# Gated cross-attention with RMSNorm: the next quad's scores behind the attention products, transposed blocks of 32 columns, two weight queues

## The chip, the cores and the metric

The kernel runs on one core of a Trainium2 chip. The core has five engines that run side by side: TensorE (matrix products), VectorE, ScalarE, GpSimd, and SyncE, which only issues transfers. They share one on-chip memory (SBUF); TensorE writes its products to a small second memory (PSUM), from which VectorE and ScalarE read them. The profile calls the engines PE (with PEld for the loading of weights), DVE, ACT, POOL and SP. The metric is the device time of one execution in microseconds.

## The reference, cut to what matters

```python
# x: (8, 1024, 1024)   ctx_1024: (8, 64, 512)
# W_mem: (1024, 512)   W_gate: (1024, 2048)   b_gate, norm_w: (1024,)
memory_proj = jnp.einsum('bme,de->bmd', memory, W_mem)
scores = jnp.einsum('bnd,bmd->bnm', hidden_states, memory_proj) / jnp.sqrt(jnp.float32(D))
attn = jax.nn.softmax(scores, axis=-1)
memory_context = jnp.einsum('bnm,bmd->bnd', attn, memory_proj)
gate_input = jnp.concatenate([hidden_states, memory_context], axis=-1)
gate = jax.nn.sigmoid(jnp.einsum('bnf,df->bnd', gate_input, W_gate) + b_gate)
fused = hidden_states + gate * memory_context
return fused * jax.lax.rsqrt(jnp.mean(jnp.square(fused), -1, keepdims=True) + EPS) * norm_w
```

All is float32. The large work is the gate's product with the part of `W_gate` that meets x, called W1 (1024 x 1024): 8192 rows of x go through it. The other half, W2, meets the memory context. Since the context is attn times the projected memory, W2 is applied once to the projected memory (512 rows in all), and attention is then taken over that product.

## The kernel before, in words

The 8192 rows of x are worked in 16 quads of 512 rows (four tiles of 128); two quads make a batch (`QPB`). The kernel has a start and a main loop.

**The start.** W_mem (`wm`), the memory (`memq`), W2 (eight tiles `w2_0` to `w2_7`, the profile's `w`) and W1 (two tiles `w1_0`, `w1_1`, also `w`) are loaded. TensorE transposes the memory (`pt`, copied to `memT` by VectorE and ScalarE), then forms the projected memory transposed, `pm`, in 32 products over four steps k of W_mem's rows; `mpT` are its copies in SBUF. `mg_product` then multiplies it with W2, `pg`, in seven products of half-size blocks (a Strassen scheme of one level, the sums of blocks `w2_sum`, `mp_step`, `mg_sum` on VectorE and GpSimd). The projected memory is stored as `mpd` and `mgd[0]`, the product with W2 as `mgd[1]`; `load_mp` and `load_mg` bring each batch's part back as `mpb` and `mg`, and `add_bias` adds the gate's bias to `mg` by an accumulating transfer that GpSimd issues.

**The main loop.** A quad of x is loaded as `xq` (`load_xq`, SyncE's queue) in an order in which VectorE's transpose of 32x32 blocks gives x transposed; `transpose_x` makes the tiles `a11`, `a12`, `a21`, `a22` (row half, column half), eight instructions a quad. The product of the quad with W1 is a Strassen scheme of two levels: seven outer products in the order 1, 6, 7, 5, 4, 2, 3 (`ORDER`), each of seven inner products A, B, C, D, A (second part), E, F. One inner product takes a *slot*; a quad has 49. `outer_s` (VectorE) makes the left operands S1 to S4 of the outer level, `inner_s` (GpSimd) those of the inner level, tile `l2`, the profile's `l`, in two buffers and two parts for each outer product. The right operands, sums of blocks of W1, are made once (`outer_sum`, `inner_sum`: tiles `t`, `it`). Inner products are evacuated to `u` and `gate` by VectorE (`fin`), ScalarE (copies) and GpSimd (`pre`).

The scores of a quad (`scores`) are 16 pairs of products in 64-column tiles, `psT` in PSUM bank `sc`; ScalarE copies them to `sT`, TensorE transposes them (`transpose_scores`), `softmax_a` and `softmax_b` make the softmax, and `transpose_attn` turns it to `attnT`. The last four outer products (5, 4, 2, 3) have an attention block between their second A and E: eight pairs of products in 64-row tiles, whose one half gives the context (`pc`), and whose other half adds the gate's part from the context to the inner products A, F, E and D. Then follow sigmoid (ScalarE), `gated` (VectorE), `residual` (an accumulating transfer issued by GpSimd), `square` (ScalarE), `norm` (VectorE) and the store.

**What sets the order.** Each engine works its instructions in the order in which they were written (`pin` keeps it). The order is written out by hand: `at(slot, ...)` puts a call ahead of the inner product of that slot, `mid((q, o), ...)` puts it behind the attention block of outer product o of quad q, ahead of E. `plan(q)` does this for a quad:

```python
at(t0 + 7, scores, q)
at(t0 + 7, outer_s, q, 3)
at(t0 + 7, outer_s, q, 4)
at(t0 + 9, transpose_scores, q)
```

So the scores of quad q stood between the outer products 1 and 6 of the quad itself. S3 overwrites `a21`, which the scores read. SyncE's and GpSimd's queues are in order too: an instruction that waits holds up what is written behind it.

Of the kernel before, what the change touches and what calls it, by code (L numbers as in the profile page):

```python
# [15 lines left out]
P = 128  # L16
# [4 lines left out]
def tile_gated_cross_attention_rmsnorm(  # L21
# [7 lines left out]
    norm_w: bass.AP,  # L29
    out: bass.AP,  # L30
):

# [28 lines left out]
    nc = tc.nc  # L64
    B, N, D = x.shape
    M, E = mem.shape[1:]
    QT = 4 * P
    QPB = N // QT
    NQ = B * QPB
    BM = B * M  # L70
    KD = D // P
    KE = E // P
# [9 lines left out]
    apool = ctx.enter_context(tc.tile_pool(name="apool", bufs=1))  # L82
    rot = ctx.enter_context(tc.tile_pool(name="rot", bufs=2))
    small = ctx.enter_context(tc.tile_pool(name="small", bufs=1))
# [4 lines left out]
    pin = tc.keep_in_program_order  # L89

    def mm(o, lhsT, rhs, start, stop):
        pin(nc.tensor.matmul(o, lhsT, rhs, start=start, stop=stop, skip_group_check=True))  # L92

    def tt(eng, o, a, b, op):
        pin(eng.tensor_tensor(o, a, b, op))  # L95

    def load(o, i):
        pin(nc.sync.dma_start(o, i))

    def t4k(pool, shape, tag, name):  # L100
        return pool.tile(shape, F32, tag=tag, name=name)

    def rows_by_chunk(w, n):

        return w.rearrange("(p j) f -> p j f", j=n)

    def chunks(t, n):

        return t.rearrange("p s e -> p (s e)").rearrange("p (m j) -> p j m", j=n)

    banks = [f"b{i}" for i in range(5)]

    def bank(n, shape, name):
        return ps.tile(shape, F32, tag=banks[n % 5], name=name)
# [11 lines left out]
    wm = t4k(xqpool, [P, KE, D], "xq", "wm")  # L126
# [3 lines left out]
        load(memq[g], memr[g])  # L130
    load(wm[:, 1, :], wmr[:, 1, :])
    load(wm[:, 2:, :], wmr[:, 2:, :])
    w2r = rows_by_chunk(w_gate_t[D:, :], KD)
    w2 = []
    for k in range(KD):
        t = t4k(*((gpool, [P, D], "gate") if k < 7 else (apool, [P, D], "s4")), f"w2_{k}")
        load(t, w2r[:, k, :])
        w2.append(t)

    w1 = [const.tile([P, 4, D], F32, name=f"w1_{h}") for h in range(2)]
    for h in range(2):
        load(w1[h], rows_by_chunk(w_gate_t[:D, :], KD)[:, 4 * h : 4 * h + 4, :])
    nw_sb = const.tile([P, D], F32, name="nw_sb")
    load(nw_sb, norm_w.partition_broadcast(P))
    xq = {}
# [17 lines left out]
    def w1_place(o):  # L165

        if o in (5, 6, 4):
            outer_b[o] = const.tile([P, 4, H], F32, tag=f"t{o}", name=f"t{o}")
        inner_t[o] = const.tile([P, 3, 2, C], F32, tag=f"it{o}", name=f"it{o}")
# [17 lines left out]
    def transpose_mem(g):  # L187

        cols = slice(g * (BM // 2), (g + 1) * (BM // 2))
        for k in range(KE):  # L190
            for r in range(2):
                n = 2 * g + r
                pin(
                    nc.tensor.transpose(
                        pt[k][:, n * P : (n + 1) * P], memq[g][:, r, k * P : (k + 1) * P], ident
                    )
                )
            o = memT[k // 2][:, k % 2, cols]
            pin((nc.scalar.copy if k % 2 else nc.vector.tensor_copy)(o, pt[k][:, cols]))

    pt = [bank(4, [P, BM], "pt0")]
    pt += [ps_ctx.tile([P, BM], F32, tag="ctx", name=f"pt{k}") for k in (1, 2)]
    pt += [ps.tile([P, BM], F32, tag="sc", name="pt3")]
    for g in range(2):
        transpose_mem(g)
    pm = [bank(j, [P, BM], f"pm{j}") for j in range(5)]
    pm += [ps_ctx.tile([P, BM], F32, tag="ctx", name=f"pm{j}") for j in (5, 6)]
    pm += [ps.tile([P, BM], F32, tag="sc", name="pm7")]
    for k in range(KE):
        for j in range(KD):  # L210
            mm(
                pm[j],
                chunks(wm[:, k : k + 1, :], KD)[:, j],
                memT[k // 2][:, k % 2, :],
                k == 0,
                k == KE - 1,
            )


    def outer_sum(o, a, b, k=slice(0, 4)):  # L220
        tt(nc.vector, outer_b[o][:, k], outer_b[a][:, k], outer_b[b][:, k], ALU.subtract)

    def inner_sum(eng, o, n):
        s, a, b = ((T1, R12, R11), (T2, R22, T1), (R12, R22, R12), (T4, R21, T2))[n]
        tt(eng, w_op(o, s), w_op(o, a), w_op(o, b), ALU.subtract)

    def inner_sums(eng, o):
        w1_place(o)
        for n in range(4):
            inner_sum(eng, o, n)  # L230
# [3 lines left out]
    A, S, L2, O = {}, {}, {}, {}  # L234
# [4 lines left out]
    def transpose_x(q, t, half):  # L239

        key = q, t // 2, half
        if key not in A:
            A[key] = t4k(
                apool, [P, KH, 2 * P], f"a{t // 2 + 1}{half + 1}", f"a{t // 2 + 1}{half + 1}_{q}"
            )
        r = t % 2
        pin(
            nc.vector.transpose(  # L248
                A[key][:, :, r * P : (r + 1) * P],
                chunks(xq[q][:, 4 * t : 4 * t + 4, :], KD)[:, half * KH : (half + 1) * KH],  # L250
            )
        )

# [122 lines left out]
    KH = KD // 2  # L376
# [8 lines left out]
    def w2_sum(eng, o, a, b):  # L385
        for k in range(KH):
            tt(eng, o[k], a[k], b[k], ALU.subtract)
# [1 line left out]
    w2_sum(nc.vector, t1, b12, b11)  # L389
    w2_sum(nc.vector, t2, b22, t1)  # L390
    w2_sum(nc.gpsimd, b12, b22, b12)
    w1_place(5)
    outer_sum(5, 7, 1)
    inner_sums(nc.vector, 1)


    mpT = [[t4k(apool, [P, KH, HM], f"a{r + 1}{h + 1}", f"mpT{r}{h}") for h in range(2)] for r in range(2)]
    for j in range(KD):
# [8 lines left out]
    def mp_step(eng, tag, pool, a, b, op):  # L407
        t = t4k(pool, [P, KH, HM], tag, f"mp_{tag}")
        tt(eng, t, a, b, op)
        return t  # L410

    def store_mp(g):

        r, n = g // 2, g % 2
        mpq = const.tile([P, 4, Q4], F32, tag=f"it{(4, 6, 2, 3)[g]}", name=f"mpq{g}")
        for h in range(2):
            pin(
                nc.vector.transpose(
                    chunks(mpq, KD)[:, h * KH : (h + 1) * KH],
                    mpT[r][h][:, :, n * P : (n + 1) * P],  # L420
                )
            )
        for i in range(4):
            load(
                mgd[0, g * P : (g + 1) * P, i * Q4 : (i + 1) * Q4].rearrange(
                    "(s c) e -> c s e", c=32
                ),
                mpq[32 * i : 32 * (i + 1), :, :],
            )
# [28 lines left out]

    s1 = mp_step(nc.vector, "s1", apool, m21, m22, ALU.add)
    s2 = mp_step(nc.vector, "s2", apool, s1, m11, ALU.subtract)  # L460
    outer_sum(7, 3, 7)
    w1_place(7)
    s3 = mp_step(nc.gpsimd, "junk", small, m11, m21, ALU.subtract)
# [9 lines left out]
    for g in (2, 3, 0, 1):  # L473
        store_mp(g)
# [4 lines left out]
    for t in range(4):  # L479
        transpose_x(0, t, 0)  # L480
# [17 lines left out]
    for t in range(2):  # L498
        transpose_x(0, t, 1)
# [7 lines left out]
    for t in (2, 3):  # L507
        transpose_x(0, t, 1)
# [11 lines left out]
    def at(slot, fn, *args):  # L520
        due.setdefault(slot, []).append(lambda: fn(*args))

    def mid(key, fn, *args):
        beside.setdefault(key, []).append(lambda: fn(*args))
# [5 lines left out]
    def plan(q):  # L530
        t0 = SLOTS * q
        nxt = q + 1 < NQ
        order = [o for o, _ in ORDER]
        for i, o in enumerate(order):
            for part, t in ((0, 1), (1, 5)):
                if i + 1 < len(order):
                    at(t0 + 7 * i + t, inner_s, q, order[i + 1], part)
                elif nxt:
                    at(t0 + 7 * i + t, inner_s, q + 1, order[0], part)
        at(t0 + 7, scores, q)  # L540
        at(t0 + 7, outer_s, q, 3)
        at(t0 + 7, outer_s, q, 4)
        at(t0 + 9, transpose_scores, q)
        at(t0 + 10, softmax_a, q)
        at(t0 + 13, softmax_b, q)
        at(t0 + 18, transpose_attn, q)
        at(t0 + 21, attn_difference, q)
        if not nxt:
            at(t0 + 5, load_last)
            return  # L550
        at(t0 + 2, load_xq, q + 1)
        for t in (2, 3):
            mid((q, 5), transpose_x, q + 1, t, 0)
            mid((q, 2), transpose_x, q + 1, t, 1)
        for i, t, half in ((36, 0, 0), (38, 1, 0), (43, 0, 1), (45, 1, 1)):
            at(t0 + i, transpose_x, q + 1, t, half)
        mid((q, 3), outer_s, q + 1, 1)
        mid((q, 3), outer_s, q + 1, 2)
        if (q + 1) % QPB == 0:
            at(t0 + 10, load_mp, (q + 1) // QPB)  # L560
            at(t0 + 49, load_mg, (q + 1) // QPB)
        if q % QPB == 0:
            at(t0 + 8, add_bias, q // QPB)

    for o in (2, 3):
        w1_place(o)
# [246 lines left out]
    for q in range(NQ):  # L813
        plan(q)
        for o, ext in ORDER:
            outer_product(q, o, ext)
# [29 lines left out]
```

## Time and profile before

| what | value |
| --- | --- |
| time, median of 3 runs | 981.03 us (980.83 to 981.19) |
| span of the profiled run | 979.4 us |
| busy: PE, DVE, POOL, ACT | 99%, 84%, 75%, 33% |
| transposes of x on DVE (L248) | 128, 1098 ns each |
| transposes mpq on DVE (L418) | 8, 1101 ns each |
| score products psT | 512 records, 58.8 us |
| attention products pc | 512 records, 127.4 us |
| weight loads: of wm for pm, of most other products | 314 ns, 190 ns |
| transfers w from in_w_gate_t, SyncE's queue | 8 of 512 KB, 2 of 2048 KB; median 11.0 and 15.6 us from issue to landing |

How to read it: each product of the program leaves two records on PE, and a product's record lasts longer than its distance to the next, since products are pipelined. So the busy share of PE says that it always had work, not how well it was used; distances between starts of records say what a product costs. The busy shares are means over the whole span. A row of a group gives busy time in all and the mean of one. Idle time of an engine that isn't on the chain that ended last costs nothing.

### The profile page before, as it was taken

What the parts mean: (1) busy time and instruction counts of PE and PEld (TensorE: products, weight loads), DVE (VectorE), ACT (ScalarE), POOL (GpSimd) and SP (SyncE); (2) the same over time, 40 slices, a digit from 0 to 9 for tenths busy, and PEclk for the clock granted to TensorE, in tenths of its full rate; (3) what the DMA queues carried; (4) which work ended last, traced back from release to release, by engine and by line L of the source; (5) the groups of instructions that cost most, each with busy time, mean ns of one, the idle gap of its engine ahead of it and who ended that gap; (6) DMA issues with size and microseconds to landing.
All of it is one profiled execution on the core that took longest, in us unless ns stands there. A gap on an engine that the chain in (4) does not pass through costs nothing.

```text
span 979.4 us, 14277 instructions
## 1 busy us (share of the span) xinstructions
PE 964.8 (99%) x4938; PEld 769.8 (79%) x4938; DVE 820.4 (84%) x1487; ACT 324.9 (33%) x602; POOL 730.5 (75%) x881
## 2 busy tenths in 40 slices
PE   9999999999999999999999999999999999999995
PEld 6546888888887888888887888888887888888873
DVE  3888788979797988979797988979797988979787
ACT  1100234151433334151433334151433334151434
POOL 3366877878787877878787877878787877878772
PEclk9999999999999999999999999999999999999998
DMA  9865264482918374482918374482818364482612
GB/s 372 258 153 145 39 120 107 103 188 62 186 65 165 108 141 106 102 190 65 183 65 164 111 138 105 107 184 66 182 65 168 110 136 104 108 184 68 169 65 86
DMA packets 71255, 128.32 MB, mean 131 GB/s; under 512 B 12432, under 2 KB 49296, under 8 KB 70928
## 3 DMA queue, kind: packets, MB, share of 16 engines
q1 hardware_dynamic: 61760, 93.34, 35.3%
q0 software_dynamic: 9280, 33.56, 18.5%
q8 instruction: 39, 0.64, 0.3%
q10 hardware_dynamic: 144, 0.52, 0.2%
q14 instruction: 32, 0.26, 0.1%
HBM read 87.56 MB, written 39.85 MB: 130 GB/s over the span
## 4 chain that ended last, share of the span: by engine, by line
PE 96%; DVE 2%; DMA 1%; issue 0%; ACT 0%; POOL 0%; DVEq 0%; ACTq 0%
PE kA L92 20%; PE pc L92 12%; PE kE L92 11%; PE kF L92 10%; PE kD L92 10%; PE kC L92 10%; PE kB L92 10%; PE psT L92 6%; PE pg L92 5%; PE pm L92 3%; DVE gate L95 1%; DMA memq<-in_mem 1%; DVE gate L660 0%; PE pa L342 0%; PE sc L316 0%
## 5 line engine op out<-in xcount | busy, mean ns | idle before, releaser
L95 POOL TENSOR_TENSOR gate<-gate,u 128x256 f32<-128x256 f32 x336 | 270.4, 835 | 115.7 <-DVE u L95 110.1
L582 ACT ACTIVATE gate<-gate 128x512 f32<-128x512 f32 x128 | 79.0, 629 | 400.1 <-DVE gate L95 400.1
L95 POOL TENSOR_TENSOR l<-a 128x256 f32<-128x256 f32 x128 | 128.9, 1007 | 60.4 <-DVE a L95 55.8
L248 DVE STREAM_TRANSPOSE a<-xq 128x512 f32<-128x512 f32 x128 | 137.9, 1098 | 4.0 <-DMA xq<-in_x 4.0
L92 PE MATMUL pc<-mg,attnT 64*128 64x256 f32 x512 | 127.4, 389 | 0.0
L611 DVE SCALAR_TENSOR_TENSOR gate<-gate,ss,nw_sb 128x512 f32<-128x512 f32 x120 | 126.0, 1060 | 1.1
L92 PE MATMUL kD<-it,l 128*128 128x256 f32 x448 | 115.0, 379 | 0.0
L92 PE MATMUL kB<-it,l 128*128 128x256 f32 x448 | 115.0, 379 | 0.0
L92 PEld LDWEIGHTS pc<-mg,attnT 64*128 64x128 f32 x512 | 90.6, 186 | 29.7 <-issue 21.2
L92 PE MATMUL kA<-w,a 128*128 128x256 f32 x384 | 98.7, 379 | 0.4 <-ACT u L726 0.4
L92 PEld LDWEIGHTS kD<-it,l 128*128 128x128 f32 x448 | 85.1, 190 | 11.6
L92 PEld LDWEIGHTS kB<-it,l 128*128 128x128 f32 x448 | 85.1, 190 | 11.6
L95 DVE TENSOR_TENSOR gate<-gate,pc 128x512 f32<-128x512 f32 x128 | 87.0, 680 | 5.8 <-ACT gate L582 5.8
L95 POOL TENSOR_TENSOR l<-s 128x256 f32<-128x256 f32 x96 | 75.7, 789 | 10.8 <-PE kF L92 10.7
L92 PEld LDWEIGHTS kA<-w,a 128*128 128x128 f32 x384 | 71.6, 190 | 10.2 <-ACT u L726 0.8
L726 ACT COPY u<-kA 128x256 f32<-128x256 f32 x112 | 40.5, 362 | 102.1 <-PE kA L92 99.9
L92 PE MATMUL kE<-it,a 128*128 128x256 f32 x256 | 69.0, 392 | 0.0
L95 DVE TENSOR_TENSOR u<-u,kB 128x256 f32<-128x256 f32 x112 | 45.5, 406 | 28.1 <-PE kB L92 24.9
L92 PE MATMUL kA<-t,s 128*128 128x256 f32 x256 | 67.4, 386 | 0.0
L92 PE MATMUL kC<-w,l 128*128 128x256 f32 x256 | 65.7, 379 | 0.0
L92 PE MATMUL kF<-w,l 128*128 128x256 f32 x256 | 65.7, 379 | 0.0
L596 ACT ACTIVATE junk<-gate 128x1024 f32<-128x1024 f32 x60 | 63.5, 1059 | 2.1 <-DMA gate<-in_x 1.2
(123 smaller groups left out, 1996.6 us busy)
## 6 DMA issues: line engine op xcount, KB each, us to landing
xq<-in_x SPq DMA_DIRECT2D x64, 512.0 KB, 9.6
gate<-in_x POOLq DMA_DIRECT2D x60, 512.0 KB, 7.8
out<-gate SPq DMA_DIRECT2D x60, 512.0 KB, 2.6
w<-in_w_gate_t SPq DMA_DIRECT2D x8, 512.0 KB, 11.0
w<-in_w_gate_t SPq DMA_DIRECT2D x2, 2048.0 KB, 15.6
mg<-mgd SPq DMA_DIRECT2D x16, 256.0 KB, 4.0
mpd<-mpT SPq DMA_DIRECT2D x4, 512.0 KB, 3.8
mgd<-mpq SPq DMA_DIRECT2D x16, 128.0 KB, 2.6
```

Of the source, the lines that this page charges most:

```text
L92: pin(nc.tensor.matmul(o, lhsT, rhs, start=start, stop=stop, skip_group_check=True))
L95: pin(eng.tensor_tensor(o, a, b, op))
L248: nc.vector.transpose(A[key][:, :, r * P : (r + 1) * P], chunks(xq[q][:, 4 * t : 4 * t + 4, :], KD)[:, half * KH : (half + 1) * KH],)
L582: pin(nc.scalar.activation(g, g, AF.Sigmoid))
L596: nc.scalar.activation(junk, O[q, t], AF.Square, accum_out=ss[:, t % 2 : t % 2 + 1])
L611: nc.vector.scalar_tensor_tensor(g[:, cols], g[:, cols], rstd[:, t % 2 : t % 2 + 1], nw_sb[:, cols], ALU.mult, ALU.mult,)
L726: pin(nc.scalar.copy(p1, kb["A"]))
```

## The change

It has three parts, and some moves of the sums around them.

1. *Scores.* The scores of quad q + 1 are computed behind the attention block of outer product 3 of quad q, so that the products in 64-column tiles follow those in 64-row tiles without full-size products between. Quad 0 keeps the old place. S3 and S4 move to slots 4 and 16 (they no longer need to follow the scores at slot 7), `add_bias` to slot 4, and the last two transposes of x from slots 43, 45 to 42, 43.
2. *Blocks of 32 columns.* The block transposes took every eighth column; now they take 32 columns in a row, and the rows of W1 and W2 are loaded in the order that fits. The projection needs W_mem's columns in that order too, so VectorE copies W_mem to four tiles `wmp` in the new order, from which TensorE reads packed weights.
3. *Two queues.* Each tile of W1 and W2 is loaded in four transfers of 32 partitions, two by SyncE's and two by GpSimd's queue. A one-column copy on GpSimd (`warm`) makes its transfers wait until W_mem's second part has landed. The sums for the right operands of the outer products 5 and 1 move behind the first sums of the projected memory.

```diff
-    def rows_by_chunk(w, n):
-        return w.rearrange("(p j) f -> p j f", j=n)
-    def chunks(t, n):
-        return t.rearrange("p s e -> p (s e)").rearrange("p (m j) -> p j m", j=n)
+    def rows_by_chunk(w):
+        return w.rearrange("(i j r) f -> i r j f", i=4, r=32)
+    def by_queue(o, w, j):
+        for i in range(4):
+            eng = nc.sync if i < 2 else nc.gpsimd
+            pin(eng.dma_start(o[32 * i : 32 * (i + 1)], w[i][:, j, :]))
...
+    warm = t4k(small, [P, 1], "warm", "warm0")
+    pin(nc.gpsimd.tensor_copy(warm, wm[:, 1, 0:1]))
...
-        load(t, w2r[:, k, :])
+        by_queue(t, rows_by_chunk(w_gate_t[D:, :]), k)
...
-        load(w1[h], rows_by_chunk(w_gate_t[:D, :], KD)[:, 4 * h : 4 * h + 4, :])
+        by_queue(w1[h], rows_by_chunk(w_gate_t[:D, :]), slice(4 * h, 4 * h + 4))
...
+    def order_wm(k):
+        t = t4k(apool, [P, KD, P], ("a11", "a12", "a21", "a22")[k], f"wmp{k}")
+        pin(
+            nc.vector.tensor_copy(
+                t.rearrange("p j (i r) -> p j i r", r=32),
+                wm[:, k, :].rearrange("p (i j r) -> p j i r", i=4, r=32),
+            )
+        )
+        wmp.append(t)
+    order_wm(0)
...
     for g in range(2):
         transpose_mem(g)
+    for k in range(1, KE):
+        order_wm(k)
...
-                chunks(wm[:, k : k + 1, :], KD)[:, j],
+                wmp[k][:, j, :],
...
-                A[key][:, :, r * P : (r + 1) * P],
-                chunks(xq[q][:, 4 * t : 4 * t + 4, :], KD)[:, half * KH : (half + 1) * KH],
+                A[key][:, :, r * P : (r + 1) * P].rearrange("p j (s c) -> p s j c", c=32),
+                xq[q].rearrange("p s (j r) -> p s j r", r=32)[
+                    :, 4 * t : 4 * t + 4, half * KH : (half + 1) * KH, :
+                ],
...
     w2_sum(nc.gpsimd, b12, b22, b12)
-    w1_place(5)
-    outer_sum(5, 7, 1)
-    inner_sums(nc.vector, 1)
...
     s2 = mp_step(nc.vector, "s2", apool, s1, m11, ALU.subtract)
+    w1_place(5)
+    outer_sum(5, 7, 1)
+    inner_sums(nc.vector, 1)
     outer_sum(7, 3, 7)
...
-        at(t0 + 7, scores, q)
-        at(t0 + 7, outer_s, q, 3)
-        at(t0 + 7, outer_s, q, 4)
+        if q == 0:
+            at(t0 + 7, scores, q)
+        at(t0 + (4 if q else 7), outer_s, q, 3)
+        at(t0 + (16 if q else 7), outer_s, q, 4)
...
-        for i, t, half in ((36, 0, 0), (38, 1, 0), (43, 0, 1), (45, 1, 1)):
+        for i, t, half in ((36, 0, 0), (38, 1, 0), (42, 0, 1), (43, 1, 1)):
             at(t0 + i, transpose_x, q + 1, t, half)
+        mid((q, 3), scores, q + 1)
...
-            at(t0 + 8, add_bias, q // QPB)
+            at(t0 + (4 if q else 8), add_bias, q // QPB)
```

The `mpq` transposes are changed in the same way as those of x.

More of the change, by code (lines that the diff above doesn't have):

```diff
@@ L132, in tile_gated_cross_attention_rmsnorm @@
     load(wm[:, 2:, :], wmr[:, 2:, :])
-    w2r = rows_by_chunk(w_gate_t[D:, :], KD)
+    warm = t4k(small, [P, 1], "warm", "warm0")
+    pin(nc.gpsimd.tensor_copy(warm, wm[:, 1, 0:1]))
     w2 = []
@@ L199, in transpose_mem @@
             pin((nc.scalar.copy if k % 2 else nc.vector.tensor_copy)(o, pt[k][:, cols]))
+    wmp = []
+    def order_wm(k):
[8 more added lines that the diff above has]
+    order_wm(0)
     pt = [bank(4, [P, BM], "pt0")]
@@ L418, in store_mp @@
                 nc.vector.transpose(
-                    chunks(mpq, KD)[:, h * KH : (h + 1) * KH],
-                    mpT[r][h][:, :, n * P : (n + 1) * P],
+                    mpq.rearrange("p s (j r) -> p s j r", r=32)[:, :, h * KH : (h + 1) * KH, :],
+                    mpT[r][h][:, :, n * P : (n + 1) * P].rearrange("p j (s c) -> p s j c", c=32),
                 )
```

## The prediction

> **What bounds the kernel now.** I read the busy shares first, then a table of stretches, then the chain that ended last, and then TensorE's timeline around one change of quad.
>
> ```profile
> PE 964.8 (99%) x4938; PEld 769.8 (79%) x4938; DVE 820.4 (84%) x1487; ACT 324.9 (33%) x602; POOL 730.5 (75%) x881
> PE 96%; DVE 2%; DMA 1%; issue 0%; ACT 0%; POOL 0%; DVEq 0%; ACTq 0%
> ```
>
> The first line is busy time by engine, the second the chain's shares. Both name TensorE. The stretches (length, then PE busy and its instructions) show where it is not full:
>
> ```profile
> 0.00:8.64 8.64, 6.38 (x27) 4.98 (x27) 1.73 (x5) 2.40 (x4) 0.74 (x7) 1.00 0.77 283
> 8.64:36.36 27.72, 27.72 (x65) 20.20 (x66) 15.55 (x21) 2.93 (x8) 9.17 (x5) 1.00 0.91 366
> 36.36:84.43 48.07, 48.07 (x114) 21.28 (x113) 41.98 (x40) 1.56 (x4) 28.31 (x21) 1.00 0.61 159
> 84.43:145.84 61.41, 61.28 (x326) 50.19 (x327) 49.79 (x93) 15.41 (x31) 47.37 (x58) 1.00 0.53 101
> 145.84:920.09 774.25, 774.25 (x4177) 635.30 (x4177) 664.50 (x1235) 276.36 (x504) 612.74 (x750) 1.00 0.55 126
> ```
>
> From 8.64 to 920 us TensorE is without a gap except 0.13 us in the first quad. So no transfer and no other engine costs anything there today: the time can fall only if TensorE's own stream gets shorter, and it rises if something makes TensorE wait. A quad takes 55.05 us (score blocks start at 310.98 and 366.02 in the chain). The stream holds hidden losses, which the timeline shows (start, length, operation; first around an attention block, then around the scores):
>
> ```profile
> 355.10 1.03 PE L92 MATMUL kA<-w,s 128*128 128x256 f32 x4
> 356.06 0.48 PE L92 MATMUL pc<-mg,attnT 64*128 64x256 f32 x1
> 356.38 0.38 PE L92 MATMUL pc<-mg,attnT 64*128 64x256 f32 x1
> 357.99 1.13 PE L92 MATMUL kE<-it,s 128*128 128x256 f32 x4
> 358.95 1.03 PE L92 MATMUL kF<-w,l 128*128 128x256 f32 x4
> 365.00 1.03 PE L92 MATMUL kF<-w,l 128*128 128x256 f32 x4
> 365.95 3.67 PE L92 MATMUL psT<-a,mpb 128*64 128x256 f32 x32
> 369.56 1.13 PE L92 MATMUL kA<-t,s 128*128 128x256 f32 x4
> 370.52 1.03 PE L92 MATMUL kB<-it,l 128*128 128x256 f32 x4
> ```
>
> Full products of four records follow each other every 0.863 us. Attention runs in two 64-row tiles, 8 pairs of records 0.215 us apart (1.72 us). From kA at 355.10 to kF at 358.95 are 3.85 us; 2 x 0.863 + 1.72 = 3.45, so 0.40 us are lost, 0.20 at each side of the block. The scores run in two 64-column tiles: kF at 365.00 to kB at 370.52 is 5.52 us; 2 x 0.863 and 16 pairs at 0.215 (3.44) make 5.17, so 0.35 us are lost, about 0.18 at each side.
>
> [...] 0.18 to 0.20 us at every change of tile shape, none inside a block. [...] The transposes of before read fp32 with a step of 32 bytes and take 1098 ns for 512 elements; weights read with that step load in 314 ns against 190 ns packed[...]. [...]
>
> **Scores behind attention.** In the changed program the 32 score records of quads 1 to 15 stand right behind the attention block of product 3 of the quad before and ahead of its E product; quad 0 stays. Before: full to rows, rows to full, full to columns, columns to full: 0.20 + 0.20 + 0.18 + 0.18 = 0.75 us. After: full to rows, rows to columns, columns to full, three changes. No row shows rows to columns. Bounds: nothing (saves 0.375 us), or as dear as the two changes it replaces (saves nothing). I take one ordinary change: a quarter of 0.75, 0.19 us a quad, 15 x 0.19 = 2.8 us.
>
> Does it bring a wait? The scores at about 357.9 need all eight transposes of the next quad. Even in the old order the last of them runs on VectorE from 355.11 to 356.21, and the change moves the last two from slots 43, 45 to 42, 43. The second half is needed 1.7 us later still, so the margin is 1.7 to 3 us. The bank "sc" was left by the attention transposes some 30 slots earlier, and the next keys are loaded from slot 10 on. No wait.
>
> E and F of product 3 now end 3.6 us later (363.3 instead of 359.8). Their buffer of inner sums is what GpSimd needs for product 6's. Today GpSimd does these at 360.67 to 365.5 (with two residual transfers between); in the new order from 363.3: two sums 1.5 us, in every second quad the bias transfer 0.85, residuals about 2.0, third sum 1.0: 368.7. Product 6 wants the third sum with its C at about 371.1. The margin is 2.4 us, smaller than before but there. The bias transfer, now at slot 4, waits for the load of mg, issued when the attention ends (303.08 in another quad) with 4.0 us to landing; GpSimd reaches it later than that. If it did block, the inner sums of product 6 stand behind it.
>
> S3 and S4 go from slot 7 to slots 4 and 16. VectorE loses the wait for the scores, 23.2 us over 16 quads (1.47 us in this one), and S3's 1.22 us fits the pauses of product 1 (0.22, 0.87 and 0.44 us). ScalarE's score copy finds ScalarE idle. None of it is on the path: worth 0.
>
> **Blocks of 32 columns.** 136 transposes now at 1.10 us [...] I take 0.65. VectorE gains about 8 x 0.45 = 3.6 us a quad, all beside TensorE: worth 0. The price is four copies of W_mem, 128x1024 each. No row has that form: the nearest, a sum of two inputs of that size (mp_s, 1.23 us), bounds it above, half of it, for one input, below; I take 1.1. The first stands ahead of VectorE's copies of the transposed memory. Its data, 0.74 us plus 4.6 to landing, is there at 5.3 to 5.8, so it ends at 6.4 to 6.9 against 6.68, when VectorE begins the next copy: 0 to 0.3 us later. Copies 2 to 4 follow from 9 to 13 us, and TensorE needs them at 15.5, 22.4 and 29.3. In return the pm stretch has 27.72 us for 64 records; at the 0.429 us of pg (48.07 / 112) it would be 27.47: 0.25 back at most. Sum 0. ScalarE's last four pm copies wait for the last pm product, since their tile lies on the fourth copy of W_mem: its end goes from 37.2 to about 37.8; the sums for the product at 43.1 end at 40.3.
>
> **W2 and W1 by two queues.** GpSimd issues 20 transfers after W_mem's second part has landed (1.8 + 7.0 = 8.8 us). Its transfer rows cost 847 and 948 ns; at 0.95 the 16 of W2 are issued by 24.0 and all by 27.8. Landing took 7.8 us for GpSimd's transfers of 512 KB, so W2 is there by 31.8 at the latest. VectorE must start on the pm copies by about 35 for TensorE's 36.36; the last W2 sum ends by 33.6. W1 lands by about 28 + 10 = 38; the changed order asks for it at 40 (product 5's and 1's sums have moved behind the pm sums). Behind the transfers on GpSimd stand its own W2 sums, 6.8 us, done by 35, wanted at 63.7.
>
> The tightest place is VectorE after 40.3: moved sums 4.75 us, outer sum 2.2, mpq transposes 7.7, two mg sums 1.25, four x transposes 4.1, then 1.2 + 3.3 + 1.2 and the four sums on b21, 6.8: 72.8 us if transposes stay at their old price. TensorE wants the last of these at 70.53 + 3 x 0.86 = 73.1. At 0.65 us they end about 4 us sooner. No wait: worth 0.
>
> Sum: 981.0 - 2.8 = 978.2 us.
>
> **The rivals.**
> - A change from rows to columns is free, as both halve the array: 15 x 0.375 = 5.6, 975.4 us. Against it: [...] that each side of a block costs the same.
> - It costs as much as the two it replaces, or the start gives 1 to 2 us back (the W_mem copy at its dear end): 980 to 981, no change.
> - A new wait, slower: GpSimd's inner sums miss product 6 (margin 2.4 us, and GpSimd is busy 75% of the time). A wait of 0.5 us each quad costs 15 x 0.5 = 7.5 less the 2.8 gained: 985.7. Or W2 comes late through GpSimd's queue and TensorE waits about 5 us at 36: 983.2. Against both: each deadline above is met at the dear end of its bounds.
>
> **How the numbers follow.** One change saved 0.66, both saved 0.10, no change 0.12, new wait 0.12. The likeliest gives 978.2. Faster is the first two, 0.76; same 0.12; slower 0.12. The range goes from the free change, 975.4, to 981.0, where the no-change case ends, and leaves out the new waits.
>
> **What would show it.** The scores' records begin about 0.2 us after the last attention pair, the next kE follows 3.6 us later, and 15 quads take 54.86 us instead of 55.05, still without TensorE idle time. VectorE's transposes fall to about 0.65 us and its wait on the scores goes. The first product of quad 0 starts at 84.4 give or take 0.3. I am wrong if the quads keep 55.05 us, if TensorE shows waits for GpSimd's l tiles or VectorE's a tiles, or if the pg stretch starts after 37 us.

## The result, and the profile after

The changed kernel takes 1003.56 us (median; 1001.69 to 1004.3) against 981.18 us before: a ratio of 1.0225, 95% interval 1.021 to 1.024. It is slower by 22.4 us; the forecast was 978.2. The profiled spans, 1000.7 and 979.4 us, differ by 21.3.

Busy time by engine and the shares of the chain that ended last, after:

```profile
PE 971.7 (97%) x4938; PEld 758.3 (76%) x4938; DVE 799.5 (80%) x1491; ACT 326.8 (33%) x602; POOL 726.4 (73%) x902
PE 71%; DVE 15%; issue 6%; POOL 4%; DMA 2%; SPq 1%; ACT 0%; DVEq 0%; POOLq 0%; ACTq 0%
```

TensorE had 96% of the chain before and has 71% now. VectorE and GpSimd have less work than before (820.4 and 730.5 us), and yet stand in the chain: not their load has grown, but TensorE now waits for them. The same stretches as in the prediction, with their bounds moved by the later start (length, then PE busy and its instructions). The bounds don't fall exactly on the phases: the product with W2 itself begins at 35.6 us (36.2 before) and the first product of quad 0 at 87.3 us (84.3 before).

```profile
8.64:37.04 28.40, 28.40 (x68) 12.62 (x67) 12.70 (x19) 2.57 (x8) 16.89 (x25) 1.00 1.04 259
37.04:87.00 49.96, 47.40 (x110) 20.17 (x109) 40.48 (x44) 1.17 (x2) 30.96 (x21) 1.00 0.78 207
87.00:148.90 61.90, 59.66 (x332) 47.78 (x331) 46.41 (x87) 10.90 (x23) 43.75 (x55) 1.00 0.49 94
148.90:941.00 792.10, 783.01 (x4175) 635.83 (x4173) 648.55 (x1240) 283.50 (x514) 602.09 (x755) 1.00 0.56 123
```

TensorE, which had one gap of 0.13 us, is idle for 2.56 us in the product with W2 (the second line), for 2.24 in the first quad and for 9.09 in the others. What ended these gaps (us in all, how many times, the longest):

```profile
PE kC L91 <- POOL l L94: 7.0, 15, 0.5
PE kB L91 <- DVE gate L94: 4.2, 8, 2.2
PE pg L91 <- DVE w L94: 2.6, 4, 0.9
```

The list counts only part of it. Where TensorE's stream stops, the first product after the stop has a record of 1.13 instead of 1.03 us and the next follows about 0.10 us later than usual. Measured from the starts of the records, against the distances of before, the delays over the quads sum to 10.7 us at kC of outer product 5 (15 quads) and 5.0 us at kB of outer product 6. Quads 1 to 14 take 56.12 us on the average instead of 55.05: 15.1 us. The scores of quad 0 begin 3.06 us later than before, quad 0 itself takes 2.2 more, and the last quad 1.0.

**The saving is there.** TensorE around the attention of outer product 3 (start, length, operation):

```profile
589.25 1.03 PE L91 MATMUL kA<-w,s 128*128 128x256 f32 x4
590.21 0.48 PE L91 MATMUL pc<-mg,attnT 64*128 64x256 f32 x1
...
591.83 0.38 PE L91 MATMUL kD<-mg,attnT 64*128 64x256 f32 x1
592.14 3.67 PE L91 MATMUL psT<-a,mpb 128*64 128x256 f32 x32
595.74 1.13 PE L91 MATMUL kE<-it,s 128*128 128x256 f32 x4
596.71 1.03 PE L91 MATMUL kF<-w,l 128*128 128x256 f32 x4
```

From kA to kF are 7.46 us; two full products (1.726), the attention (1.72) and the scores (3.44) make 6.89. So three changes of tile shape cost 0.57 us, 0.19 each, as the forecast took it. One by one it is the same: from the start of the attention to what follows it are 1.93 us, whether kE follows (before) or the scores (now), and from the start of the scores to the next product 3.61 before and 3.60 now. The change from rows to columns costs what any other does, and a quad saves 0.19.

**The first wait: outer product 5.** VectorE, GpSimd and TensorE in the 5 us ahead of a wait for GpSimd:

```profile
614.11 0.41 DVE L94 TENSOR_TENSOR u<-u,kB 128x256 f32<-128x256 f32 x1
614.44 1.21 DVE L94 TENSOR_TENSOR s<-a,s 128x1024 f32<-128x1024 f32 x1
...
615.58 0.41 DVE L94 TENSOR_TENSOR u<-u,kC 128x256 f32<-128x256 f32 x1
...
615.91 0.41 DVE L94 TENSOR_TENSOR u<-u,kD 128x256 f32<-128x256 f32 x1
616.12 2.10 POOL L94 TENSOR_TENSOR gate<-gate,u 128x256 f32<-128x256 f32 x3 [2.48 <-DVE u L94]
...
618.18 0.72 POOL L94 TENSOR_TENSOR l<-s 128x256 f32<-128x256 f32 x1
...
618.95 1.13 PE L91 MATMUL kC<-t,l 128*128 128x256 f32 x4 [0.47 <-POOL l L94]
```

The second line is S4, at its new slot 16. It lies between VectorE's sums u from kB and from kC. GpSimd sat idle for 2.48 us until these u were there, did its three sums of `pre`, and only then the inner sum l that kC of product 5 needs; TensorE waits 0.47 us. S4 itself runs in its normal time: a sum of 1.21 us in the wrong place is passed on through two engines.

**The second wait: outer product 6.**

```profile
601.45 1.05 POOL L94 TENSOR_TENSOR l<-s 128x256 f32<-128x256 f32 x1
601.56 2.70 DVE L94 TENSOR_TENSOR a<-a,a 128x1024 f32<-128x1024 f32 x1
...
602.14 1.03 POOL L94 TENSOR_TENSOR l<-s,l 128x256 f32<-128x256 f32 x1
...
604.19 0.41 DVE L94 TENSOR_TENSOR gate<-u,kD 128x256 f32<-128x256 f32 x1
...
604.75 1.10 PE L91 MATMUL kB<-it,l 128*128 128x256 f32 x4
```

S3, at slot 4, takes 2.70 us instead of the 1.22 it took before, and VectorE's evacuation of kD stands behind it; kB of product 6 uses that PSUM bank and comes 0.26 to 0.46 us late. GpSimd's two sums run from 601.45 to 603.17, and 603.17 + 1.22 = 604.39 is about where S3 ends (604.26): as if it had begun when they were done. No run here takes GpSimd's sums away, but three traces (before, after, and the scores-alone kernel below) hold both cases: where no sum of GpSimd's runs beside it, S3 or S4 always takes 1.21 to 1.23 us (44 times) and a norm 0.74 to 0.75 (52 times); beside GpSimd's sums they take up to 2.9 and 4.8 us. What holds them up is not shown.

**What had been lost.** VectorE of before, at the old place of the scores:

```profile
367.95 1.22 DVE L95 TENSOR_TENSOR a<-a,a 128x1024 f32<-128x1024 f32 x1 [1.47 <-PE psT L92]
369.09 1.22 DVE L95 TENSOR_TENSOR s<-a,s 128x1024 f32<-128x1024 f32 x1
371.66 0.42 DVE L95 TENSOR_TENSOR u<-u,kB 128x256 f32<-128x256 f32 x1 [1.35 <-PE kB L92]
```

For 3.6 us, from 365.95 on, TensorE made scores, which ask VectorE for nothing. S3 ran in that time, S4 just behind it, and 1.35 us of waiting were still left. This pause now lies behind the attention of product 3, where VectorE waits for E (3.23 us in one quad). The forecast booked the vanished wait for the scores as time won by VectorE; it was the place in which S3 and S4 cost nothing.

### The profile page after: what moved, and what is told of

The parts are those of the page before. It is cut to its first block, busy times and chain, and to the rows that moved or that the text cites. A ratio compares the mean times of both kernels' runs of the same rounds, so it can differ in the third digit from the quotient of the medians.

```text
span 1000.7 us, 14380 instructions
## 1 busy us (share of the span) xinstructions
PE 971.7 (97%) x4938; PEld 758.3 (76%) x4938; DVE 799.5 (80%) x1491; ACT 326.8 (33%) x602; POOL 726.4 (73%) x902
## 4 chain that ended last, share of the span: by engine, by line
PE 71%; DVE 15%; issue 6%; POOL 4%; DMA 2%; SPq 1%; ACT 0%; DVEq 0%; POOLq 0%; ACTq 0%
PE kA L91 13%; PE pc L91 11%; PE kE L91 8%; PE kC L91 8%; PE kB L91 7%; PE kD L91 7%; PE kF L91 6%; PE psT L91 6%; DVE gate L633 4%; DVE gate L94 3%; PE pm L91 3%; POOL gate L94 3%; DVE u L94 3%; PE pg L91 2%; DMA out<-gate 2%
## 5 line engine op out<-in xcount | busy, mean ns | idle before, releaser
L94 POOL TENSOR_TENSOR gate<-gate,u 128x256 f32<-128x256 f32 x336 | 284.3, 877 | 144.1 <-DVE u L94 138.0
L91 PE MATMUL kB<-it,l 128*128 128x256 f32 x448 | 117.4, 384 | 4.9 <-DVE gate L94 4.2
L94 POOL TENSOR_TENSOR l<-a 128x256 f32<-128x256 f32 x128 | 99.5, 778 | 25.7 <-DVE a L94 16.1
L94 DVE TENSOR_TENSOR gate<-gate,kE 128x256 f32<-128x256 f32 x112 | 45.5, 418 | 70.7 <-PE kE L91 65.5
L91 PEld LDWEIGHTS kB<-it,l 128*128 128x128 f32 x448 | 82.7, 190 | 23.9 <-issue 7.9
L267 DVE STREAM_TRANSPOSE a<-xq 128x512 f32<-128x512 f32 x128 | 85.9, 692 | 8.2 <-issue 8.2
L94 DVE TENSOR_TENSOR u<-u,kB 128x256 f32<-128x256 f32 x112 | 46.2, 412 | 29.2 <-PE kB L91 22.7
L94 DVE TENSOR_TENSOR gate<-gate,kF 128x256 f32<-128x256 f32 x112 | 46.1, 419 | 27.7 <-PE kF L91 20.3
## 6 DMA issues: line engine op xcount, KB each, us to landing
w<-in_w_gate_t POOLq DMA_DIRECT2D x4, 512.0 KB, 15.1
```

The source lines that it names most:

```text
L267: nc.vector.transpose(A[key][:, :, r * P : (r + 1) * P].rearrange("p j (s c) -> p s j c", c=32), xq[q].rearrange("p s (j r) -> p s j r", r ...
```

## The experiments

Each was measured beside the kernel before, which took 980.77 to 980.85 us.

**Scores alone.** Before, with part 1's scores and nothing else of the change:

```diff
-        at(t0 + 7, scores, q)
+        if q == 0:
+            at(t0 + 7, scores, q)
...
+        mid((q, 3), scores, q + 1)
```

> Kernel before, with only the scores moved behind the attention block of product 3 (S3 and S4 stay at slot 7, old transposes, old loads). Theory A, the waits of the changed kernel come from the new slots of S3 and S4: quads of 54.86 us and no TensorE wait, 15 x 0.19 us saved, 978.3 us (977.6 to 979.2). Rival R, the waits come from the scores' new place itself (E and F of product 3 end 3.6 us later, GpSimd falls behind): kB of product 6 and kC of product 5 wait here too, about 1 us a quad, 994 to 998 us.

1022.26 us, ratio 1.0423 (1.0409 to 1.0437): worse than the whole change, and outside both theories; no wait at kB of product 6 is left, but another place was hit. Every second quad takes 58.7 to 61.6 us, the others 55.6. In the long ones kB of product 7 waits about 3.7 us for VectorE, whose norm there shows 4.68 us. VectorE first, then GpSimd in the same time:

```profile
209.86 4.68 DVE L613 SCALAR_TENSOR_TENSOR gate<-gate,ss,nw_sb 128x512 f32<-128x512 f32 x1
214.47 0.41 DVE L95 TENSOR_TENSOR gate<-gate,kA 128x256 f32<-128x256 f32 x1
```

```profile
209.03 0.83 POOL L372 DMA_DIRECT2D mg<-in_b_gate  x1
209.60 2.36 POOL L95 TENSOR_TENSOR gate<-gate,u 128x256 f32<-128x256 f32 x3
211.66 0.98 POOL L95 TENSOR_TENSOR l<-a 128x256 f32<-128x256 f32 x1
212.34 0.97 POOL L95 TENSOR_TENSOR l<-a,l 128x256 f32<-128x256 f32 x1
213.02 0.97 POOL L95 TENSOR_TENSOR l<-s 128x256 f32<-128x256 f32 x1
```

The norm (1.06 us on the average before) ends only 0.5 us after the six sums of GpSimd shown here, which run without a gap and had piled up behind the bias transfer at slot 8. That transfer is issued once in two quads.

**S3 and S4 put back in the changed kernel**, first S4 alone, then both:

```diff
-        at(t0 + (4 if q else 7), outer_s, q, 3)
-        at(t0 + (16 if q else 7), outer_s, q, 4)
+        at(t0 + (4 if q else 7), outer_s, q, 3)      # first; 7 in the second
+        at(t0 + 7, outer_s, q, 4)
```

> Changed kernel with S4 put back to slot 7 (S3 stays at slot 4). Theory A: S4 at slot 16 stands ahead of VectorE's u sums of product 7, GpSimd's sums wait for these, and the inner sums of product 5 behind them come late; with S4 away the wait of kC in product 5 (15 times 0.62 to 0.74 us and about 0.1 of restart, 12 us) is gone: 991.5 us (989.5 to 994), and the 0.3 to 0.4 us wait of kB in product 6 stays. Rival R: kC waits as before, 1002 to 1005 us.

> Changed kernel with S3 and S4 both at slot 7. Theory A: S3 at slot 4 meets GpSimd's inner sums (2.7 instead of 1.2 us) and holds up the sum that frees the PSUM bank of product 6's B; with both away, both waits (12 and 6.5 us) are gone: 985 us (983 to 988), what is left being the start (3.1), quad 0 (2.4) and the end. Rival R: both waits stay, 1000 to 1005 us.

995.01 us (1.0144, 1.013 to 1.0158) and 996.07 (1.0169, 1.0155 to 1.0183). With S4 back the delay at product 5 goes from 10.7 to 1.8 us. With S3 back too the delay at product 6 goes, but the time does not fall to the 985 us that were expected: both sums at slot 7 bring small new waits (0.18 us at kB of product 7, 0.25 at kC of product 5, nearly every quad). So each wait belongs to its own sum, and slot 7 has no room for both any more.

**S4 alone, in the kernel before.** The scores stay in their old place:

```diff
-        at(t0 + 7, outer_s, q, 4)
+        at(t0 + (16 if q else 7), outer_s, q, 4)
```

> Kernel before with S4 alone put to slot 16, the scores at their old place. If S4's slot is enough for the wait of kC in product 5 (GpSimd's third inner sum for it ends 328.6, TensorE asks at about 328.9 today, a margin of 0.3 us against 1.2 us of S4): 0.8 to 0.9 us in each of 16 quads, 993 us (990 to 996). If the wait needs the scores' new place as well: 980.5 to 982 us.

993.47 us, ratio 1.0128 (1.0113 to 1.0143): 12.6 us from one line. The waits of TensorE from 60 us on:

```profile
PE kC L92 <- POOL l L95: 7.0, 15, 0.5
PE kA L92 <- ACT u L726: 1.7, 3, 1.1
```

The first line is that of the changed kernel, to the tenth. Slot 16 is bad by itself; it needs neither the new place of the scores nor the new transposes nor the new start.

**S4 at slot 30**, in the changed kernel with S3 at 7, and in the kernel before with the scores moved:

```diff
+        at(t0 + (30 if q else 7), outer_s, q, 4)
```

> Changed kernel with S3 at slot 7 and S4 at slot 30. Theory B: at the scores' old place VectorE and GpSimd had 3.6 us ahead of product 6 in which TensorE needed nothing from them; without it they run so tight from product 1 to product 5 that any VectorE sum of 1.2 us put there makes TensorE wait. At slot 30 the packed transposes have left room, so S4 costs nothing there: no wait of kB or kC is left, quads of 54.9 us instead of 55.7 with S3 and S4 both at slot 7, 983.5 us (982 to 987). Rival S: GpSimd's own row of sums is what comes late, whatever VectorE does: quads stay at 55.6 and more, 994 to 997 us.

> Kernel before with the scores moved and S4 at slot 30 (old transposes, old loads, S3 and bias as before). Theory B: with S4 out of product 6's stretch the wait of kB in product 7 is gone in both kinds of quads: 978.5 us (977.8 to 981). Rival T: the long waits of every second quad come from the bias transfer at slot 8[...]; S4 does not matter to it and they stay: 1005 to 1020 us.

993.45 us (1.014, 1.0116 to 1.0164) and 1011.19 (1.028, 1.0234 to 1.0326; three executions took 1010 to 1012 us, one 1002.6). Both are well above what theory B expected. In both, every second quad takes 54.87 to 54.95 us: the saving. The others do not. With the bias at slot 4 they take 55.35 to 56.35: a square on ScalarE waits for a residual transfer that GpSimd issued behind the bias transfer, and ScalarE's copy of kA, which frees TensorE's bank, stands behind it:

```profile
220.31 1.06 ACT L618 ACTIVATE junk<-gate 128x1024 f32<-128x1024 f32 x1 [3.40 <-DMA gate<-in_x]
```

With the bias at slot 8 they take 59.2 to 59.6, with the wait at product 7 as above.

**The bias transfer at slot 5**, in three kernels: scores moved, S3 and S4 at 7; scores moved, S4 at 30; the changed kernel with S3 at 7 and S4 at 30 (where the line had 4 instead of 8 from quad 1 on):

```diff
-            at(t0 + 8, add_bias, q // QPB)
+            at(t0 + (5 if q else 8), add_bias, q // QPB)
```

> Kernel before with the scores moved and the bias transfer at slot 5; S3 and S4 at slot 7. If the long waits of every second quad come from the bias transfer at slot 8: they are gone, all quads take 55.6 us as the odd ones do, 989.5 us (988 to 992). If not: 1015 to 1022 us, as with the scores alone.

> Kernel before with the scores moved, S4 at slot 30 and the bias transfer at slot 5, behind GpSimd's inner sums for product 6 (old transposes, old loads). Theory B, with the bias transfer the cause of what is left in every second quad: all quads take 54.9 us as the odd ones of the run with the bias at slot 8 do, 978.4 us (977.8 to 979.6). Rival U: in every second quad the squares then wait for the residual transfer, which has 3.6 us less to land, and ScalarE's copy for product 5 comes late: 0.5 to 1.2 us in 7 quads, 982 to 987 us.

> Changed kernel with S3 at slot 7, S4 at slot 30 and the bias transfer at slot 5. Theory B: the quads take 54.9 us; what is left over the kernel before is the start with its two queues (0 to 3 us) and quad 0 (2.2 us) less 2.7 for the scores: 981 to 984 us. Rival U: every second quad keeps about 1 us (squares waiting for the residual): 988 to 992 us.

989.81 us (1.0091, 1.0077 to 1.0105), 981.99 (1.001, 1.0001 to 1.0018) and 985.94 (1.0051, 1.0037 to 1.0065). Against the same kernels with the bias at slot 8 (scores alone: 1022.26; with S4 at 30: 1011.19) the place of this one issue is worth 32 and 29 us; against slot 4 (993.45) 7.5 us. The second of these kernels was run once more, and the trace told below is of this run:

> The kernel before with the scores behind attention, S4 at slot 30 and the bias at slot 5, once more, for a trace of it: the time is expected at 981 to 983 us as in the first run of it. It was worked out at 978.4 (54.87 us a quad). Theory F: something outside the quads' plan gives 3.6 us back, at the start or in quad 0: then quads 1 to 14 take 54.86 to 54.95 us each and the start or quad 0 is longer by about 3 us. Theory G: the gain is real in some quads only, and others wait 0.3 to 0.6 us for the squares that stand behind a residual transfer, as in the quads that begin a batch in the run with S4 at slot 30: then every second quad takes 55.2 to 55.5 us.

982.11 us (1.0014, 1.0008 to 1.0021). Eleven of quads 1 to 14 take 54.88 to 55.00 us, three 55.4 to 55.6: the mean is again 55.05. So the gain is real in some quads and lost in others (theory G). The start is not longer (the scores of quad 0 begin at 90.10 us against 90.40); from the last scores to the end are 71.95 us, 1.17 more than in the fastest kernel below. One of the long quads, VectorE and TensorE:

```profile
228.28 1.42 DVE L95 TENSOR_TENSOR s<-a,s 128x1024 f32<-128x1024 f32 x1
...
229.62 0.68 DVE L95 TENSOR_TENSOR gate<-gate,pc 128x512 f32<-128x512 f32 x1
...
230.34 0.48 PE L92 MATMUL pc<-mg,attnT 64*128 64x256 f32 x1 [0.25 <-DVE gate L95]
```

S4 stands ahead of the gate's product, which frees the bank of pc, and the attention of product 4 is 0.74 us late.

**S3 at slot 4 alone; S4 at slot 33**, each against the kernel just told:

```diff
+        at(t0 + (4 if q else 7), outer_s, q, 3)      # one kernel
+        at(t0 + (33 if q else 7), outer_s, q, 4)     # the other
```

> The kernel of the run beside it, with S3 at slot 4 in place of 7 from quad 1 on, nothing else. Theory: S3 at slot 4 alone makes the second product of outer product 6 (kB) wait for VectorE's evacuation of product 1, 0.33 us and 0.10 us of restart in each of 15 quads, so 6.5 us more than the run beside it: about 988.5 us. Rival: the wait needs the changed layout or S4 at slot 16 beside it; then S3's slot is worth nothing as the prediction said, and the time is that of the run beside it, 982.

> The kernel of the first run of this call with S4 at slot 33 in place of 30 (S4 is wanted by product 4's inner sums; nothing else moves). If S4 at slot 30 still costs TensorE something (it stands ahead of VectorE's evacuations of product 4's neighbours), the time falls towards 978.4 us; if the quads already run at 54.9 us, or if what is left comes from the start or the squares, it stays within 0.5 us of the first run. If S4 comes too late for the sums of product 4, the time rises by 0.3 us or more a quad, to 986 or above.

986.98 us (1.0062, 1.0047 to 1.0077) and 986.93 (1.0059, 1.0043 to 1.0076), both 4.8 to 4.9 us above it. S3 at slot 4 costs that without the new layout and without S4 at slot 16: the wait at product 6 is there (S3 took 2.72 us), somewhat cheaper than expected. S4 at slot 33 costs more than at slot 30; which wait does it isn't worked out here.

**S3 into the new pause.** Before, with the scores moved, the bias at slot 5, S4 at its old slot 7, and S3 of the next quad right behind its scores; the second kernel has S4 at slot 24:

```diff
+        if q == 0:
+            at(t0 + 7, outer_s, q, 3)
+        at(t0 + 47, outer_s, q + 1, 3)
         at(t0 + 7, outer_s, q, 4)      # (24 if q else 7) in the second
```

> The kernel before with the scores behind attention, the bias at slot 5, S4 at its old slot 7, and S3 of the next quad at slot 47 of the quad before: right behind the scores, where the trace shows VectorE idle for 2.2 us until the products E and F of outer product 3 are there. Theory H: each sum that VectorE makes elsewhere in the first two outer products of a quad costs a wait because the scores' pause is no longer there, and the only free place for it is the pause itself, where it has moved to; S3 (1.2 us) then fits there without delay, S4 alone at slot 7 causes no wait (none for product 5's kC was seen with S4 at 7), and the quads take 54.86 to 54.95 us: 978.0 to 979.5 us. Rival: S3 collides with GpSimd's sums for product 1 of the next quad, takes 2.7 us as it did at slot 4, and the evacuation of E comes late: a wait of 0.3 us or more a quad at product 1, 983 us or above. Rival 2: the gain of 0.19 us a quad is again lost in quads whose norms stand close together, 981 to 982.

> The kernel of the run beside it with S4 at slot 24 from quad 1 on. If S4 at slot 7 still leaves waits in product 7 (kB, 0.18 us a quad) this one is faster by up to 2.7 us; if slot 24 is as tight as slots 16 and 33 were (transposes of x and norms follow at the attention of product 5), it is slower by 5 us or more.

The first takes 978.59 us, ratio 0.998 (0.9972 to 0.9987): faster than both kernels, by 2.2 us against before (its slowest execution, 980.14, is quicker than the quickest of before, 980.66). From the kernel with both sums at slot 7 and the bias at slot 5 (989.81 us) it differs in nothing but the place of S3, which is thus worth 11.2 us; and S4 alone at slot 7 brings none of the waits that the two brought there together. The second takes 985.72 (1.0053, 1.0039 to 1.0067), so slot 24 is no free place for S4 either. VectorE of the first, behind the scores:

```profile
194.02 0.41 DVE L95 TENSOR_TENSOR gate<-gate,kD 128x256 f32<-128x256 f32 x1
194.35 1.77 DVE L95 TENSOR_TENSOR a<-a,a 128x1024 f32<-128x1024 f32 x1
197.16 0.42 DVE L95 TENSOR_TENSOR gate<-gate,kE 128x256 f32<-128x256 f32 x1 [1.04 <-PE kE L92]
```

S3 takes 1.77 us, and VectorE still waits 1.04 us for E: it costs nothing there. The waits of TensorE in the list are those of before, and quads 1 to 14 take 54.90 us on the average.

**The start.** Parts 2 and 3 alone, with the loop's order as before (the transposes at their old slots too):

```diff
-        if q == 0:
-            at(t0 + 7, scores, q)
-        at(t0 + (4 if q else 7), outer_s, q, 3)
-        at(t0 + (16 if q else 7), outer_s, q, 4)
+        at(t0 + 7, scores, q)
+        at(t0 + 7, outer_s, q, 3)
+        at(t0 + 7, outer_s, q, 4)
...
-        mid((q, 3), scores, q + 1)
...
-            at(t0 + (4 if q else 8), add_bias, q // QPB)
+            at(t0 + 8, add_bias, q // QPB)
```

> Changed kernel with the scores, S3, S4, the bias and the last two transposes back at their old slots: blocks of 32 columns and two queues alone. Theory B: quads of 55.05 us as before; the start loses 0 to 3 us and quad 0 about 2.2: 983 to 986 us. If the packed transposes helped TensorE, or the new order of the weights hurt it: quads off 55.05 us.

986.37 us, ratio 1.0055 (1.004 to 1.0069). Quads 1 to 14 take 55.05 us, as before, so transposes of 692 instead of 1098 ns bring nothing; the scores of quad 0 begin at 92.93 us and quad 0 takes 59.19 instead of 55.37 us. Two kernels, both the changed one without `warm`, test the loads. One has all transfers of W1 and W2 on SyncE's queue, still of 32 partitions; the other has whole transfers of 128 partitions there, in the new row order:

```diff
-            eng = nc.sync if i < 2 else nc.gpsimd
-            pin(eng.dma_start(o[32 * i : 32 * (i + 1)], w[i][:, j, :]))
+            pin(nc.sync.dma_start(o[32 * i : 32 * (i + 1)], w[i][:, j, :]))   # one
+        load(o, w[:, :, j, :])                                                # the other
```

> Changed kernel with all transfers of W1 and W2 by SyncE's queue, still of 32 partitions each, and without the one-column copy that held GpSimd's back. Theory P1, the transfers of 32 partitions make the weights slow whoever issues them: the start loses at least as much as in the changed kernel (scores of quad 0 at 93.5 us or later), 1003 to 1007 us. Rival P2, GpSimd's queue makes them late: the scores of quad 0 start at 90.5 us again, 1000.5 us (999 to 1001.5).

> Changed kernel with W2 and W1 in the same new row order, but each slice by one transfer of 128 partitions on SyncE's queue, none by GpSimd. Theory P1, transfers of 32 partitions are slow: the rate after 11 us goes from 200 to 300 back to above 380 GB/s, scores of quad 0 start at 90.3 us (give or take 0.4), the time falls by what the start lost, to 1000.5 us (999.5 to 1001.5). Rival: the new row order is slow to read; the rate stays under 300 GB/s and the scores of quad 0 start after 93 us, 1003 us and more.

1007.15 us (1.027, 1.0256 to 1.0284) and 1048.74 (1.07, 1.0683 to 1.0718). The stretch from 20 to 28 us of before, of the changed kernel, and of these two (the last two columns are the busy share of the DMA engines and GB/s):

```profile
20.00:28.00 8.00, 8.00 (x20) 5.85 (x19) 4.89 (x4) 0.00 (x0) 4.63 (x3) 1.00 1.02 431
```

```profile
20.00:28.00 8.00, 8.00 (x20) 3.51 (x19) 2.63 (x4) 0.00 (x0) 3.66 (x7) 1.00 1.05 249
```

```profile
20.00:28.00 8.00, 8.00 (x20) 3.50 (x19) 2.69 (x4) 0.00 (x0) 4.12 (x3) 1.00 1.05 229
```

```profile
20.00:28.00 8.00, 8.00 (x20) 3.49 (x19) 1.38 (x2) 0.00 (x0) 0.00 (x0) 1.00 0.26 104
```

In transfers of 32 partitions the DMA engines are as busy as before (1.05 against 1.02) and move little more than half (249 and 229 against 431 GB/s). The second queue isn't to blame: without it the scores of quad 0 begin 4.6 us later still (98.08 against 93.46). The two queues, which write to both halves of the partitions at once, gain only 20 GB/s over the one. What makes these transfers slow isn't settled: the last kernel was to tell the 32 partitions from the new row order, and it does not, since its DMA engines are only 26% busy and move 104 GB/s. Why they are so little busy is not shown either.

## Why the prediction was wrong

- **The step that failed: "None of it is on the path: worth 0", for S3 and S4 at slots 4 and 16.** S4 at slot 16 costs 12.6 us alone, S3 at slot 4 costs 4.9 alone. The step set S3's 1.22 us against three pauses of VectorE in product 1 (0.22, 0.87 and 0.44 us), none of which is as long as S3, and S3 took 2.70. It didn't look at slot 16 at all: there it should have followed VectorE's u to GpSimd's `pre` and its inner sums to kC. It counted 23.2 us of VectorE's wait for the scores as a gain, where it was the room for these sums. Putting S3 into the new pause, with S4 left at slot 7 and the bias at slot 5, brings the saving back, as the kernel of 978.59 us shows.
- **The three changes of shape**: right, 0.19 us each. The saving of 2.8 us was worked out for 15 quads; the best kernel gained 2.2 us.
- **No wait for the eight transposes**: right; the scores begin 0.31 us behind the last attention pair and no wait of psT is listed.
- **GpSimd's sums for product 6, margin 2.4 us**: TensorE doesn't wait for them, but kB waits there for VectorE. The rival "a new wait", 985.7 us, named GpSimd at product 6 and 0.5 us a quad; there were two waits, at products 5 and 6, of about 0.7 and 0.3 us a quad, and the larger one, at product 5, is not the one that the rival named.
- **The bias at slot 4**: "GpSimd reaches it later than that" was too easy. Its place is worth up to 32 us between slots 8 and 5 and, with S3 at 7 and S4 at 30, 7.5 us between 4 and 5. In the changed kernel as it is, slot 4 seems to cost little: TensorE's waits for ScalarE's copy come to 1.7 us in 3 times there (1.6 in 3 before), but to 6.6 in 9 in the kernel with S4 at 30 and the bias at slot 4. No run has this one line changed.
- **Blocks of 32 columns**: 0.65 us was taken for a transpose, the author's estimate, which no row of before gives, 0.69 measured; 1.1 for a W_mem copy, 0.69 measured, inside its bounds (1.23 us and half of it); worth 0, right.
- **Two queues**: W2 "there by 31.8" held, just (31.8). The step "W1 lands by about 28 + 10 = 38" failed: W1 landed at 46.2 us. The stores of `mpd` and the first x are transfers behind it; x is issued from 43.8 to 51.1 instead of 39.0 to 43.0 us, and its fourth part lands at 62.5 instead of 54.8. VectorE sits idle for 8.2 us (last columns; the page names no releaser) and begins the transposes of x at 62.8:

```profile
L267 DVE STREAM_TRANSPOSE a<-xq 128x512 f32<-128x512 f32 x128 | 85.9, 692 | 8.2 <-issue 8.2
```

The last of the b21 sums ends at 76.0 us where 72.8 was worked out, at the old price of the transposes, and 73.1 needed. That is 2.6 us of waits in the product with W2. Six of the kernels told here share this start, and their traces move in step: where W1 landed at 43.2 us (S4 back), the b21 sums ended at 72.7, inside the 73.1, TensorE had no wait there, and quad 0 began at 84.1, as early as before; where it landed at 46.2 (the changed kernel), 76.0 and 87.3; the other four lie between, in the same order. Why W1 lands sooner in some runs than in others isn't shown. With quad 0's wait, parts 2 and 3 cost 5.5 us alone.

The terms measured one at a time, though in different kernels, nearly add up: 12.6 + 4.9 + 5.5 - 2.2 = 20.8 of 22.4 us. The 1.6 that are left are not assigned; the start, which differs by 3 us between these traces of the same start, can hold them. Why quad 0 waits 2.2 us for VectorE is open: one sum there takes 3.73 instead of 0.68 us beside six sums of GpSimd in a row, which stand behind the bias transfer at slot 8 (quad 0 keeps it there), as in the scores-alone kernel. It does so with parts 2 and 3 alone as well; no run moves that transfer in quad 0.

## What to carry to other kernels

Moving a block of work on the bounding engine also moves the pause that this block gave the others: list what ran in the pause, and move it along. An engine at 84% has free time on the average and none in the wrong slot. So follow each moved instruction to whoever waits for what stands behind it, over two engines if need be. A cheaper instruction off the path (transposes at 0.69 for 1.10 us) bought nothing (quads of 55.05 us with either), and parts 2 and 3, which brought it, cost 5.5 us at the start and in quad 0.

## What the hardware did that was not expected

- Three of VectorE's instructions lasted until 0.5 to 1.1 us after a whole row of GpSimd's sums beside them: a norm took 4.68 us beside six sums (0.75 with none beside it), S3 2.70 beside two (1.22 with none), a sum for the right operands 3.73 beside six (0.68 with none).
- A stop of TensorE cost about 0.10 us more than its length (1.13 us for the first record, 0.97 us to the next product, against 1.03 and 0.863). The first full product behind a change of tile shape shows the same 1.13 and 0.97. In the scores-alone kernel the granted clock was 0.62 from 214 to 216 us, where a stop of 3.56 us ended (at 215.26), and 0.50 from 216 to 220 (PEclk is the last column but two):

```profile
216.00:218.00 2.00, 2.00 (x7) 1.55 (x6) 1.93 (x6) 1.60 (x3) 0.00 (x0) 0.50 0.35 141
```

- From 20 to 28 us, the transfers of 32 partitions moved 229 to 249 GB/s with the DMA engines fully busy (1.05), those of 128 partitions 431 (1.02; in another row order, which no run separates from it).
